# Attention scores of four key tiles accumulated by key differences, values held by chunk, both stored by ScalarE

## The chip, the core and the metric

The kernel runs on one core of one Trainium2 chip. The metric is the device time of one execution in microseconds (us); the median of several runs is compared. A core has TensorE (PE, the matrix multiplier, with its weight loads listed as PEld), VectorE (DVE), ScalarE (ACT), GpSimd (POOL) and SyncE (SP, which here only issues transfers). Each works through its own instructions in order. TensorE writes into banks of PSUM, of 512 fp32 numbers per partition, and may add to what a bank holds. 16 DMA engines move data between SBUF and the chip's memory.

## The reference, cut to what matters

One transformer block with a condition, for `x` of 2 batches, 2048 tokens, width 512, in fp32; 16 heads of 32:

```
mod = silu(cond) @ Wada + bada                    # six vectors per batch
xm  = layernorm(x) * (1 + sc_a) + sh_a
q, k, v = split(xm @ Wqkv)                        # 16 heads of 32
s   = where(causal, q @ k.T * 32**-0.5, -inf)
x   = x + gt_a * (softmax(s) @ v @ Wproj + bproj)
xm  = layernorm(x) * (1 + sc_m) + sh_m
x   = x + gt_m * (gelu(xm @ W1 + b1) @ W2 + b2)
```

## The kernel before, in words

The phases follow each other: QKV of batch 0, attention of batch 0, output projection of batch 0, QKV of batch 1, attention of batch 1, then a last phase with the projection of batch 1 and the MLP.

**QKV** (`Qkv.group`, L811). Tokens are worked in four groups g of 512. In a group, for each of four chunks f (four heads, 128 features) first the queries, then the keys are computed into a PSUM bank `ps_qk` (four matmuls, L823). Each result is split into a high part (ScalarE, L830) and the rest (VectorE, L831), both in a tile `hl` (four buffers), and stored by SP (L836) to scratch in DRAM; after f = 0 the keys of chunk 0 and a block of queries are loaded back (L842). Then four tiles of values `ps_v` are computed and copied by ScalarE into `vv`, which holds the values of all 2048 tokens and 16 heads (L852). `among` is called behind each matmul and sets score products between them (below). `norm` and `load_x` prepare the next group.

In batch 1's QKV, POOL also works on weights for the MLP: `Quarters.step` (L924), and after it `FirstLayer.step` (L988), which loads a room of seven blocks of 512 columns, forms four sums in it and stores it to `w1e` (two rooms, seven of them in all; `also`, L1228, calls them).

**Attention** (`attention_phase`, L541). The keys of a chunk in SBUF (`kst`) and the queries of a unit (`qst`) hold high and low parts on 128 partitions, so that one matmul with 128 rows gives the product of both. A unit is a chunk c and a block i of 512 queries; the order of blocks is 0, 1, 2, 3 in chunk 0 and 0, 2, 1, 3 in the others (L275). A step of a unit is a tile of 128 keys (L662): 4i tiles below the diagonal, then one on it, then two steps for the other three tiles on the diagonal. The exponent needs each query's maximum first. So there are two kinds of products with the keys:

- *Score products* `s` (`Row.score`, L494, through `bank`): queries on the partitions, up to 512 keys wide; VectorE takes the maximum (L461, or L456 with the causal mask). They run ahead, for units to come. They have two PSUM banks, and `score` may borrow one of `st` (`borrow`). How many a step takes is set by `due` and `count` (L675, L484) from the weights of the steps (`weight`, L668) and the costs of the products left.
- *Scores* `st` (`scores_t`, L550): keys on the partitions, 512 queries wide, one bank for each of the four heads. A step first writes minus the maximum into each bank by a small bf16 matmul, the **fold** (`sel` times `fold`, which `rows`, L516, makes), and adds keys times queries. ScalarE takes the exponent into `e` (L593); POOL zeroes what lies above the diagonal (`affine_select`, L602). The loop over the heads in `scores_t` also fixes where a step's score products stand among its scores: behind two or three of them, one more into a borrowed bank at the end.

Two steps later (`LAG`), the products of `e` with the values (`o`) follow (L729). Row sums `sm` come from products with `ones`; for tiles below the diagonal POOL first adds up to five `e` into `ee` (L623; VectorE does so in the last unit), and one product takes the sum (L736). `e` has eight tiles of two heads, `ee` four. `flush` (L656) sets values, row sums and the unit's end behind the scores of the step in which they come due.

Of the kernel before, what the change touches and what calls it, by code (L numbers as in the profile page):

```python
# [12 lines left out]
ALU = mybir.AluOpType  # L13
# [14 lines left out]
def dit_block_kernel(  # L28
# [69 lines left out]
    ones = bp.tile([P, P], F32, tag="ones", name="ones")  # L98
# [8 lines left out]
    nc.vector.tensor_scalar(sel, ones, -1.0, None, ALU.mult)  # L107
# [61 lines left out]
    ]  # L169
    n_early = (C - 1) * NQ  # L170
# [118 lines left out]
    class Row:  # L289


        def __init__(self, b):
            self.b = b
            self.vv = bp.tile([P, NT, D], F32, tag="vv", name="vv")
            self.kst, self.qst, self.pools = {}, {}, {0: bp}
            self.at = 0
# [11 lines left out]
        def load_keys(self, c, g, n=1):  # L308
# [6 lines left out]
            for r in range(4):  # L315
# [3 lines left out]
                )  # L319

# [220 lines left out]
    def attention_phase(row):  # L541
        b, vv, kst, qst = row.b, row.vv, row.kst, row.qst
        with pool(f"att{b}") as ap, pool(
# [4 lines left out]
            n_bank = [0]  # L548

            def scores_t(u, step, n):  # L550
# [21 lines left out]
                for h in range(HC):  # L572
                    g = slice(h * HD, (h + 1) * HD)
                    st = st_bank()
                    mm(
                        st[:, :w], sel[g, :], fold[u % 2][g, q0 : q0 + w],
                        start=True, stop=False,
                    )
                    sts.append(st)
                for h in range(HC):  # L580
                    at = 0
                    for j, q in tiles:
                        mm(
                            sts[h][:, at : at + QB - q],
                            kst[c][:, h, j * P : (j + 1) * P],
                            qst[u][:, h, q:],
                            start=False, stop=at + QB - q == w,
                        )
                        at += QB - q
# [94 lines left out]
            for u, (c, i) in enumerate(units):  # L684
                if NQ <= u + AHEAD < len(units):
                    row.load_queries(u + AHEAD)
                if u % NQ == 0 and c + 1 < C:
                    row.load_keys(c + 1, 0, NG)
                steps = len(steps_of[u])
                for n_step, tiles in enumerate(steps_of[u]):  # L690
                    last = n_step == steps - 1
# [37 lines left out]
                    def values(es=es, tiles=tiles, c=c, o=o, first=n_step == 0, last=last):  # L729
                        tile_by_tile(  # L730
                            o,
                            lambda j, h: vv[:, j, (c * HC + h) * HD : (c * HC + h + 1) * HD],
# [3 lines left out]
                    def row_sums(es, last, tiles=((0, 0),), sm=sm, summed=summed):  # L736
                        first = not summed
                        summed.add(len(summed))
                        tile_by_tile(sm, lambda j, h: ones[:, :HD], es, tiles, first, last)
# [29 lines left out]
    class Qkv:  # L769
# [41 lines left out]
        def group(self, g, hp, between, among):  # L811
# [5 lines left out]
            n = 0  # L817
# [1107 lines left out]
```

## Time and profile before

| | |
|---|---|
| median of 3 runs | 2321.45 us (2317.7 to 2322.69) |
| the profiled execution's own time | 2323.13 us |
| its span | 2321.4 us, mean granted TensorE clock 0.998 |
| PE busy | 2270.8 us (98%) |
| DVE, ACT, POOL busy | 1582.5, 914.6, 1290.9 us |
| DMA | 355.60 MB, mean 153 GB/s |
| QKV, then attention of batch 0 | about 0 to 213, 213 to 742 us |
| projection of batch 0, QKV of batch 1 | about 742 to 826, 826 to 997 us |
| attention of batch 1 | about 997 to 1533 us |
| the rest (projection of batch 1, MLP) | about 1533 to 2321 us |

The profile is of one execution. Its page lists busy times of the engines, slices of the span (a digit is tenths busy, 9 is 90% or more), and groups of instructions: line, engine, operation, tile written and tiles read, shape, count, then busy time, the mean of one in ns, and the engine's idle time just ahead of them with what ended it. A timeline lists start, duration, engine, line and operation in order of time, with the idle time before in brackets and what released it. An x4 joins four like instructions. The time of a matmul in it reaches beyond the start of the next one, since matmuls are pipelined; so the distance of starts is what one costs PE.

### The profile page before, as it was taken

The page shows a single profiled execution, that of the slowest core. Times are in us where ns is not written, and L with a number is a line of the kernel's source. Part 1 is how long each engine was busy: PE and PEld are TensorE (multiplying, and loading weights), DVE is VectorE, ACT ScalarE, POOL GpSimd, SP SyncE. Part 2 cuts the span into 40 slices and gives each one's busy share as a digit, 9 for nine tenths or more (in the row PEclk, how much of TensorE's full clock was granted, in tenths as well). Part 3 has the DMA queues.
Part 4 walks back from the last instruction along what each step waited for, and adds up shares of the span by engine and source line. Part 5 has one row for each costly group of instructions (what it writes and reads, how often), then busy time and mean ns, then how long its engine had stood idle before and what let it go on. Part 6 is the DMA issues. An engine that isn't in the chain of part 4 may idle for free. (4 is left out here: it accounts for less than half of the span.)

```text
span 2321.4 us, 33398 instructions
## 1 busy us (share of the span) xinstructions
PE 2270.8 (98%) x12141; PEld 1388.8 (60%) x12141; DVE 1582.5 (68%) x3117; ACT 914.6 (39%) x1744; POOL 1290.9 (56%) x1036
## 2 busy tenths in 40 slices
PE   8999999999999999999999999999999999999998
PEld 4455545455544444555455554446888888888887
DVE  3366776777666735677667777555896876877787
ACT  2112555555565021155555554622332152251230
POOL 1052987878793663478788886653764602602510
PEclk9999999999999999999999999999999999999999
DMA  7577216151233799981522404265375554654643
GB/s 257 185 243 204 55 28 133 29 119 47 74 115 127 241 297 298 320 235 24 113 48 48 100 24 134 81 206 205 118 279 200 199 186 146 212 173 151 216 143 116
DMA packets 118524, 355.60 MB, mean 153 GB/s; under 512 B 14496, under 2 KB 15052, under 8 KB 103640
## 3 DMA queue, kind: packets, MB, share of 16 engines
q1 hardware_dynamic: 107040, 293.64, 41.9%
q0 software_dynamic: 10944, 59.28, 7.0%
q8 instruction: 96, 1.57, 0.3%
q14 instruction: 68, 0.56, 0.1%
q10 hardware_dynamic: 376, 0.55, 0.1%
HBM read 253.80 MB, written 107.48 MB: 156 GB/s over the span
## 5 line engine op out<-in xcount | busy, mean ns | idle before, releaser
L593 ACT ACTIVATE e<-st 128x512 f32<-128x512 f32 (+1 forms) x1152 | 573.1, 579 | 411.6 <-PE st L203 350.5
L461 DVE TENSOR_REDUCE mx<-s 128x1 f32<-128x512 f32 x604 | 408.0, 687 | 185.0 <-PE s L203 183.6
L623 POOL TENSOR_TENSOR ee<-ee,e 128x1024 f32<-128x1024 f32 x212 | 498.8, 2385 | 8.3 <-ACT e L593 8.3
L203 PE MATMUL s<-kst,qst 128*128 128x512 f32 (+3 forms) x1032 | 466.5, 453 | 15.9 <-DVE mx L461 6.3
L203 PE MATMUL st<-qst,kst 128*128 128x512 f32 (+3 forms) x1280 | 410.1, 387 | 0.0
L203 PE MATMUL ps_a<-sum,room 128*128 128x256 f32 x1504 | 357.4, 382 | 6.6 <-DVE c L1409 3.8
L203 PEld LDWEIGHTS ps_a<-sum,room 128*128 128x128 f32 x1504 | 281.5, 190 | 56.0 <-issue 8.7
L203 PE MATMUL o<-e,vv 128*32 128x512 f32 (+3 forms) x2560 | 300.8, 539 | 0.8 <-POOL e L602 0.8
L203 PEld LDWEIGHTS s<-kst,qst 128*128 128x128 f32 x1032 | 194.5, 189 | 174.0 <-DVE mx L461 58.6
L456 DVE CUSTOM_DVE_ANT_0 junk<-s,causal 128x512 bf16<-128x512 f32 (+3 forms) x428 | 209.2, 489 | 126.2 <-PE s L203 118.7
L203 PEld LDWEIGHTS st<-qst,kst 128*128 128x128 f32 x1280 | 227.5, 188 | 96.8 <-issue 66.7
L623 POOL TENSOR_TENSOR ee<-e 128x1024 f32<-128x1024 f32 x84 | 198.4, 2384 | 130.5 <-ACT e L593 130.4
L203 PE MATMUL ps_qk<-xmT,wqkv 128*128 128x512 f32 x512 | 240.5, 597 | 1.8 <-DVE xmT L263 1.8
L602 POOL TENSOR_SCALAR_AFFINE_SELECT e<-e 128x256 f32<-128x256 f32 x256 | 103.8, 436 | 107.2 <-ACT e L593 74.2
L203 PEld LDWEIGHTS ps_qk<-xmT,wqkv 128*128 128x128 f32 x512 | 94.2, 190 | 97.7 <-issue 91.4
L1637 POOL TENSOR_TENSOR c<-c,h 128x512 f32<-128x512 f32 x40 | 58.2, 1474 | 160.8 <-ACT c L1635 160.8
L203 PE MATMUL ps_b<-sum,room 128*128 128x256 f32 x608 | 143.6, 379 | 0.0
L203 PEld LDWEIGHTS ps_b<-sum,room 128*128 128x128 f32 x608 | 115.0, 190 | 15.4
L203 PE MATMUL ps_v<-wqkv,xmT 128*128 128x512 f32 x256 | 122.3, 594 | 0.0
L203 PEld LDWEIGHTS o<-e,vv 128*32 128x32 f32 x2560 | 60.8, 108 | 101.1 <-issue 83.4
L203 PE MATMUL st<-fold,sel 32*128 32x512 bf16 (+1 forms) x1152 | 116.1, 372 | 3.6 <-DVE mhl L482 2.6
L461 DVE TENSOR_REDUCE mx<-st 128x1 f32<-128x512 f32 x164 | 112.7, 687 | 4.9 <-PE st L203 2.7
(179 smaller groups left out, 2869.6 us busy)
## 6 DMA issues: line engine op xcount, KB each, us to landing
qst<-q SPq DMA_DIRECT2D x128, 256.0 KB
room<-w1e SPq DMA_DIRECT2D x28, 1024.0 KB
kst<-k SPq DMA_DIRECT2D x24, 1024.0 KB
room<-w1e SPq DMA_DIRECT2D x28, 768.0 KB
room<-w2e SPq DMA_DIRECT2D x21, 1024.0 KB
q<-hl SPq DMA_DIRECT2D x32, 512.0 KB
k<-hl SPq DMA_DIRECT2D x32, 512.0 KB
room<-w2e SPq DMA_DIRECT2D x21, 768.0 KB
```

What stands on the lines that cost most here:

```text
L203: return tc.keep_in_program_order(nc.tensor.matmul(*args, **kw))
L456: nc.vector.tensor_tensor_reduce(junk[:, :w], s[:, :w], causal[:, QB - w :], 1.0, MASKED, ALU.add, ALU.max, m,)
L461: nc.vector.tensor_reduce(m, s[:, :w], axis=AX.X, op=ALU.max)
L593: act(nc.scalar.activation(e[:, h % 2, :w], sts[h][:, :w], AF.Exp))
L602: nc.gpsimd.affine_select(d, d, pattern=[[0, 2], [1, P]], compare_op=ALU.is_ge, fill=0.0, base=0, channel_multiplier=-1,)
L623: act(engine.tensor_tensor(dst, x, y, ALU.add))
L1637: nc.gpsimd.tensor_tensor(c, c, piece_of(base, i, t, pair), ALU.add)
```

## The change

Four consecutive key tiles of a 512-key group, below the diagonal, now use the same four banks `st`. The first of the four steps writes the fold and the scores as before. The other three add only (next keys − keys before) times the queries onto the bank that is still there, and so turn the scores of one tile into those of the next, with the maximum already in. Such a step (`by_difference`) has no fold.

- The differences are made in QKV: for g < 3 and each chunk, ScalarE copies 384 columns of the keys' PSUM bank, VectorE subtracts them from the following 384 in the bank, and the difference is split in high and low (`dl`, in the buffers of `hl`, now five) and stored to new scratch `dd` by ScalarE, one tile later. `load_differences` brings them back by SP: those of chunk 0 at the end of each group, those of chunk c + 1 in steps 6, 10 and 14 of the last unit of chunk c.
- The values are held by chunk, in two buffers: chunk 0 is copied in QKV, the other 384 columns go through a tile `vt` (two buffers) to scratch `vd`, stored by ScalarE, and are loaded for the next chunk in the third unit of a chunk.
- The score products of a step with differences stand elsewhere: the first one (with three or more) ahead of its scores, that is, right behind the values of the step before. They borrow no bank, and the step before a step with differences borrows none either. The fixed part of such a step's weight is 800 instead of 1250.
- `ones` has 32 columns; `sel` is made from the identity.
- FirstLayer works in 14 halves of rooms, in three buffers, one call at every n instead of every second one; Quarters' rooms in that stage are three single ones.

The diff, cut to its core:

```
+    dd = [[dram.tile([2, P, NG - 1, MT - P], F32, ...) for c in range(C)] for b in range(B)]
+    vd = [dram.tile([P, NT, D], F32, tag=f"v{b}", name=f"v{b}") for b in range(B)]
...
+        def load_differences(self, c, g):
+            t = bp.tile([P, HC, MT - P], F32R, tag=f"dst{g}", name="dst")
+            for r in range(4):
+                nc.sync.dma_start(
+                    t[r * HD : (r + 1) * HD].bitcast(F32),
+                    dd[self.b][c][r % 2, :, g].rearrange("(h d) t -> d h t", d=HD),
+                )
+            self.dst[c, g] = t
...
+        def new_values(self, c):
+            self.vv[c] = bp.tile([P, NT, P], F32, tag="vv", name="vv", bufs=2)
+        def load_values(self, c):
+            self.new_values(c)
+            nc.sync.dma_start(self.vv[c], vd[self.b][:, :, c * P : (c + 1) * P])
...
+            def by_difference(u, step):
+                return step % TQ > 0 and step < units[u][1] * TQ
...
+                differ = by_difference(u, step)
+                if differ:
+                    sts = banks[0]
+                    first, *behind = {
+                        0: (0, 0, 0, 0, 0),
+                        1: (0, 0, 1, 0, 0),
+                        2: (1, 0, 1, 0, 0),
+                        3: (1, 0, 1, 0, 1),
+                        4: (1, 1, 0, 1, 1),
+                    }[min(n, HC)]
+                    row.score(first)
+                else:
...
+                    banks[0] = sts
...
+                        if differ:
+                            keys = row.dst[c, j // TQ][:, h]
+                            keys = keys[:, (j % TQ - 1) * P : j % TQ * P]
+                        else:
+                            keys = kst[c][:, h, j * P : (j + 1) * P]
                         mm(
+                            sts[h][:, at : at + QB - q], keys, qst[u][:, h, q:],
                             start=False, stop=at + QB - q == w,
+                            skip_group_check=differ,
                         )
...
-                    if h < 2 and n >= 3 or h >= HC - n and n < 3:
+                    if differ:
+                        row.score(behind[h])
+                    elif h < 2 and n >= 3 or h >= HC - n and n < 3:
                         row.score(1)
-                if n >= 3:
-                    row.score(1, st_bank)
+                if n >= 3 and not differ:
+                    row.score(1, None if by_difference(u, step + 1) else st_bank)
                     row.score(min(n, HC) - 3)
...
-                    weight.append(1250 + (12 if n < i * TQ else 14) * w // 2)
+                    fixed = 800 if by_difference(u, n) else 1250
+                    weight.append(fixed + (12 if n < i * TQ else 14) * w // 2)
...
+                if u % NQ == 2 and c + 1 < C:
+                    row.load_values(c + 1)
...
+                    if u % NQ == NQ - 1 and c + 1 < C and n_step in (6, 10, 14):
+                        row.load_differences(c + 1, n_step // TQ - 1)
...
+                    stored(n)
+                    if which and g < NG - 1:
+                        before = hp.tile([P, MT - P], F32, tag="before", name="before")
+                        act(nc.scalar.copy(before, ps[:, : MT - P]))
+                        d = ps[:, P:]
+                        act(nc.vector.tensor_tensor(d, d, before, ALU.subtract))
+                        dl = hp.tile([P, 2, MT], F32R, tag="hl", name="dl", bufs=5)
+                        dl = dl[:, :, : MT - P]
+                        act(nc.scalar.activation(dl[:, 0, :], d, AF.Copy))
+                        act(
+                            nc.vector.tensor_tensor(
+                                dl[:, 1, :], d, dl[:, 0, :].bitcast(F32), ALU.subtract
+                            )
+                        )
+                        late.append((n + 1, dl, f))
...
-                nc.scalar.copy(row.vv[:, g * MTT + t, :], ps)
+                act(nc.scalar.copy(row.vv[0][:, g * MTT + t, :], ps[:, :P]))
+                vt = hp.tile([P, D - P], F32, tag="vt", name="vt", bufs=2)
+                act(nc.scalar.copy(vt, ps[:, P:]))
+                act(nc.scalar.dma_start(vd[b][:, g * MTT + t, P:], vt))
+                stored(n)
```

`stored(n)` lets ScalarE issue the stores of `dl` that are due; `act` keeps an instruction in its place in the program's order.

More of the change, by code (lines that the diff above doesn't have):

```diff
@@ L169, in dit_block_kernel @@
     ]
+    dd = [
+        [
+            dram.tile([2, P, NG - 1, MT - P], F32, tag=f"d{b}{c}", name=f"d{b}{c}")
+            for c in range(C)
+        ]
+        for b in range(B)
+    ]
+    vd = [dram.tile([P, NT, D], F32, tag=f"v{b}", name=f"v{b}") for b in range(B)]
     n_early = (C - 1) * NQ
@@ L738, in row_sums @@
                         summed.add(len(summed))
-                        tile_by_tile(sm, lambda j, h: ones[:, :HD], es, tiles, first, last)
+                        tile_by_tile(sm, lambda j, h: ones, es, tiles, first, last)
                     pending.append((now + LAG, values))
@@ L1231, in also @@
                         quarters.step()
-                elif n % 2 == 0:
+                else:
                     late.step()
             def rooms():
-                w = hp.tile([P, 7, C * P], F32, tag="w49", name="w7", bufs=2)
-                w = w.rearrange("p n d -> p (n d)")
-                return [w[:, k * piece : (k + 1) * piece] for k in range(2)]
+                w = hp.tile([P, 7, HK * P], F32, tag="w49", name="w7", bufs=3)
+                return [w.rearrange("p n d -> p (n d)")]
             quarters.more_rooms = rooms
             qkv.run(hp, also)
-            assert quarters.at >= FC and late.at == 7 and not late.rooms
+            assert quarters.at >= FC and late.at == 14 and not late.rooms
     attention_phase(row)
```

66 lines of the change are left out of this document (41 added, 25 removed).

## The prediction

> **What bounds the kernel now.** I read the page first: its span, the busy line, the slices, the groups.
>
> ```profile
> span 2321.4 us, 33398 instructions
> PE 2270.8 (98%) x12141; PEld 1388.8 (60%) x12141; DVE 1582.5 (68%) x3117; ACT 914.6 (39%) x1744; POOL 1290.9 (56%) x1036
> POOL 1052987878793663478788886653764602602510
> ...
> L623 POOL TENSOR_TENSOR ee<-ee,e 128x1024 f32<-128x1024 f32 x212 | 498.8, 2385 | 8.3 <-ACT e L593 8.3
> L456 DVE CUSTOM_DVE_ANT_0 junk<-s,causal 128x512 bf16<-128x512 f32 (+3 forms) x428 | 209.2, 489 | 126.2 <-PE s L203 118.7
> L203 PE MATMUL st<-fold,sel 32*128 32x512 bf16 (+1 forms) x1152 | 116.1, 372 | 3.6 <-DVE mhl L482 2.6
> ```
>
> TensorE (PE) is full on average; but the slices of POOL (GpSimd) say 8 and 9 tenths for long stretches, and an average over stages hides which of the two ends last. So the windows by stage came next (attention of batch 0, projections and QKV of batch 1, attention of batch 1, then two 10 us pieces inside that QKV; columns: window and length, then PE, PEld, DVE, ACT, POOL busy with counts, granted clock, DMA share, GB/s).
>
> ```profile
> 213.00:742.00 529.00, 521.74 (x3666) 261.55 (x3665) 368.19 (x873) 303.24 (x607) 403.86 (x281) 1.00 0.32 80
> 826.00:997.00 171.00, 166.24 (x468) 82.28 (x466) 90.55 (x218) 30.75 (x55) 84.88 (x106) 0.99 0.93 313
> 997.00:1533.00 536.00, 524.55 (x3666) 262.55 (x3667) 372.16 (x875) 303.63 (x608) 408.42 (x285) 1.00 0.33 85
> ...
> 900.00:910.00 10.00, 7.17 (x16) 3.54 (x17) 6.66 (x16) 0.60 (x1) 2.39 (x3) 0.83 0.86 283
> 930.00:940.00 10.00, 10.00 (x35) 5.38 (x34) 7.50 (x22) 3.28 (x6) 6.12 (x6) 1.00 1.02 368
> ```
>
> Attention has PE busy 98% and the DMA a third busy. QKV of batch 1 is the stage without room: DMA share 0.93, and the one place where PE stops and its clock falls.
>
> The timeline of PE shows what a step of attention costs, and that of DVE (VectorE) how soon a bank of score products comes free.
>
> ```profile
> 652.33 0.39 PE L203 MATMUL st<-fold,sel 32*128 32x512 bf16 x4
> 652.65 0.50 PE L203 MATMUL st<-qst,kst 128*128 128x512 f32 x1
> 652.99 0.40 PE L203 MATMUL s<-kst,qst 128*128 128x512 f32 x1
> ...
> 653.45 0.40 PE L203 MATMUL s<-kst,qst 128*128 128x512 f32 x1
> ...
> 654.15 0.39 PE L203 MATMUL st<-kst,qst 128*128 128x512 f32 x1
> 654.38 0.40 PE L203 MATMUL s<-kst,qst 128*128 128x512 f32 x1
> 654.71 1.06 PE L203 MATMUL o<-e,vv 128*32 128x512 f32 x8
> 655.71 0.39 PE L203 MATMUL st<-fold,sel 32*128 32x512 bf16 x4
> ```
> ```profile
> 653.42 1.29 DVE L461 TENSOR_REDUCE mx<-s 128x1 f32<-128x512 f32 x2 [0.95 <-PE s L203]
> 654.63 0.68 DVE L461 TENSOR_REDUCE mx<-st 128x1 f32<-128x512 f32 x1
> 655.23 0.68 DVE L456 CUSTOM_DVE_ANT_0 junk<-s,causal 128x512 bf16<-128x512 f32 x1
> ```
> ```profile
> 643.89 0.08 DVE L456 DVE_READ_ACCUMULATOR2_ANT mx<- 128x1 f32 x1
> ...
> 644.03 0.19 PEld L203 LDWEIGHTS s<-kst,qst 128*128 128x128 f32 x1 [0.27 <-DVE mx L456]
> ```
>
> A step is 655.71 − 652.33 = **3.38 us**: 0.32 for four folds (652.65 − 652.33), matmuls 0.23 apart (654.38 − 654.15), 1.00 for values and row sums. A reduction starts 0.43 after its product (652.99 to 653.42), reductions follow each other 0.60 apart (654.63 to 655.23), and the next product starts 0.06 after the bank is read (643.97 to 644.03).
>
> **Part 1: the folds.** Steps that differ number 9, 6 and 3 in the units of query blocks 3, 2 and 1: 18 for each of 4 chunks and 2 batches, 144. A fold gone is 0.32, so 144 × 0.32 = 46 us of PE work leave. That is the ceiling. Against it stands where the score products go. By the built order of PE, 18 of the 144 lie in the last units and carry no products, 86 run product, difference, product, two differences, product, difference, product, 38 begin with two products, and 2 have three products. Ahead of differing steps, 42 fold steps end with two products in a row into the two s banks, where one went to a borrowed bank of st before. Replayed by the intervals above, every product 512 wide:
>
> - Plain differing step: products at 0, 0.46, 1.15, 1.61. The second reduction frees its bank at 0.43 + 0.60 + 0.60 + 0.06 = 1.69, so the fourth product waits 0.08. Step 3.38 − 0.32 + about 0.05 = 3.11 at worst, 3.06 without a wait: saves 0.27 to 0.32.
> - Beginning with two products: the third is wanted at 0.69 and its bank is free at 0.43 + 0.60 + 0.06 = 1.09. This and a second wait eat the 0.32 and more: −0.10.
> - The 42 fold steps: their fourth product is wanted at 2.05, its bank is free at 2.35, and more follows in the next step: −0.39.
>
> All wide: 86 × 0.27 − 38 × 0.10 − 42 × 0.39 = +3 us gained. With no bank wait: 124 × 0.32 = 40. The masked reductions (x428, mean 489 ns against the wide 0.68) are shorter; I take −0.02, −0.29 and +0.31, nearer the wide replay because the wide ones are the more: 86 × 0.31 − 38 × 0.02 − 42 × 0.29 = **14 us** that PE could gain.
>
> **Part 2: what POOL allows.** Its timelines over a unit of block 2 (first two rows, 11 steps) and one of block 3 (last three rows):
>
> ```profile
> 365.75 4.73 POOL L623 TENSOR_TENSOR ee<-e 128x1024 f32<-128x1024 f32 x2 [7.36 <-ACT e L593]
> ...
> 399.33 2.20 POOL L602 TENSOR_SCALAR_AFFINE_SELECT e<-e 128x256 f32<-128x256 f32 x6
> ...
> 437.27 9.40 POOL L623 TENSOR_TENSOR ee<-ee,e 128x1024 f32<-128x1024 f32 x4 [0.52 <-ACT e L593]
> 447.92 4.72 POOL L623 TENSOR_TENSOR ee<-e 128x1024 f32<-128x1024 f32 x2 [1.24 <-ACT e L593]
> ...
> 462.58 4.71 POOL L623 TENSOR_TENSOR ee<-e 128x1024 f32<-128x1024 f32 x2 [0.59 <-ACT e L593]
> ```
> ```profile
> 401.55 0.16 PEld L203 LDWEIGHTS o<-e,vv 128*32 128x32 f32 x8 [0.23 <-POOL e L602]
> ```
>
> In block 2 POOL runs without a gap from 365.75 to 401.53 (399.33 + 2.20; the rows between name no idle time), and at its end PE already waits 0.23 for the diagonal's selects, which stand in POOL's queue behind the adds. The adds don't change. A faster PE arrives at the same select and waits longer: **block 2 with its 48 differing steps gains nothing**. In block 3 POOL idles 0.52 + 1.24 + 0.59 = 2.35 us; only that can be taken. Six such units (the last units add on DVE) hold 6 × 2.35 = 14 us at most; I take the largest single idle of each, 1.24, since a chain's first add still waits for its own Exp: −7.4 us.
>
> Something goes back. Of the units of blocks 2 and 3, 12 have a first differing step that begins with two products. There the second head's difference comes behind the waiting third product: 0.23 × 3 + 0.40 + 0.23 + 0.06 of DVE order = about 1.38 after the values, against 652.99 + 0.23 − 652.33 = 0.89 now. POOL's first add and all behind it start 0.49 later: 12 × 0.49 = +5.9. Attention with products: −7.4 + 5.9 = **−1.5** (bounds: −14, that idle all used and nothing given back; +20, the wide losses of the 42 and 38 steps, 16.4 + 3.8, with no step's gain).
>
> **Part 3: the last units.** No products stand there, and DVE adds.
>
> ```profile
> 704.48 0.40 PE L203 MATMUL st<-fold,sel 32*128 32x512 bf16 x4
> ...
> 706.93 0.40 PE L203 MATMUL st<-fold,sel 32*128 32x512 bf16 x4
> ```
> ```profile
> 705.39 2.06 ACT L593 ACTIVATE e<-st 128x512 f32<-128x512 f32 x4 [0.39 <-PE st L203]
> ```
>
> A step is 2.45; without the fold 2.13, still over the 2.06 of ACT (ScalarE). At most 18 × 0.32 = 5.8; but the same four banks are written again, each only after its Exp, so ACT's chain nearly closes. I take **−4** (bounds −5.8 and 0).
>
> **Part 4: QKV.** Per group with g < 3 there are new: 4 ACT copies and 4 high parts of 384, 4 × 2 subtractions on DVE, 4 stores by ScalarE; per V tile a second copy and a store; then 4 loads of differences on SP. DMA per batch, by the tiles' sizes: 12 × 393 KB of differences (4.7 MB), 16 × 196 KB of values (3.1 MB), 3 × 786 KB loaded back (2.4 MB): 10.2 MB. The loads for later chunks lie in attention, at a DMA share of a third; I price them at nothing there, and at 2 us for a batch if that cover failed. FirstLayer moves the same bytes in halves, in three rooms. In batch 0 QKV the DMA has gaps and DVE is not full; I take **+2** (0 to +6).
>
> In batch 1 the cover is thin. What waits there, and for what, by the waits of that stage and the timelines of PE and POOL:
>
> ```profile
> POOL w L968 <- DMA w1e<-w: 42.2, 5, 12.7
> DVE stat L215 <- DMA x<-in_x_dram: 13.7, 6, 4.7
> SPq L316 <- DMA k<-hl: 17.3, 3, 10.3
> ...
> ACT hl L830 <- DMA k<-hl: 0.9, 1, 0.9
> ```
> ```profile
> 902.83 0.50 PE L203 MATMUL s<-kst,qst 128*128 128x512 f32 x1 [3.17 <-DVE mx L461]
> ```
> ```profile
> 1000.54 0.58 POOL L996 DMA_DIRECT2D w1e<-w  x1 [0.30 <-POOL w L963]
> 1001.13 2.28 POOL L602 TENSOR_SCALAR_AFFINE_SELECT e<-e 128x256 f32<-128x256 f32 x6
> ```
>
> One late x tile stops DVE, in whose queue the reductions stand behind it; so PE stands for 3.17 us, and runs the 10 us around it at clock 0.83 (another 1.7). The stores of differences stand ahead of such loads on the same DMA engines: 313 GB/s × 171 us are 53.5 MB, so 10.2 MB is 19% more traffic, and each of the 6 late x tiles comes later by about that share of 10 us, SP's longest wait here, taken as the age of a transfer that queues: 6 × 1.9 = 11, of which I let a third reach PE, as 3.17 + 1.7 of 13.7 did: +4. The buffer hl serves 12 tiles of a group in place of 8: five buffers for a tile each 2.5 us instead of four for one each 3.76, 12.5 us of cover instead of 15, while SP stands up to 10.3 us before it can store: +2. POOL's rooms end 0.6 us ahead of the attention's first selects; the same traffic stretches them: +3. Together **+9** (0, if DMA and DVE hide all, to +29, under the rivals).
>
> On the stores: the row of the DMA share says 1.02 at 930. The Trainium skill (DMA: Bandwidth & Descriptors, section Issuing engines are not separate DMA queues) says that transfers of all issuing engines run on the same 16 DMA engines and interleave, so that another issuer saves only issue time. By it, storing from ScalarE spares SP 28 issues a batch and nothing on the engines; were it otherwise, the +4 for x would be 0. No run here shows it yet.
>
> MLP: unchanged, 0.
>
> **Sum:** −1.5 − 4 + 2 + 9 = +5.5 on the profiled execution's 2323.13: 2328.6. That execution lies 1.7 above the median of the shown runs (2321.45), so the median to expect is **2327**.
>
> **Rivals.**
> *Faster: PE's bound is the real one.* The banks do not bind and POOL's idle is used: 6 × 2.35 + 5.8 in the last units = 20, less 2 for QKV, where gaps of the DMA hide the rest: 2321.45 − 18 = 2303. For it: masked reductions are short, POOL has 125 us idle in the 529. Against: those lie at units' starts, and 401.55 shows POOL ending last. Chance 0.27.
> *Slower: DMA in QKV of batch 1.* 10.2 MB at 368 GB/s take 28 us, and a share of 0.93 leaves 0.07 × 171 = 12: 16 over. When a tile in hl lives over 12.5 us (SP's 10.3 and the landing), ACT stops, with it DVE and the products: 3 groups × 4.5 = 13. It decides from the point where landings pass 2.2 us behind SP's longest wait. −5.5 + 2 + 29 = +25.5: 2347. For it: 1.02 at 930. Against: 0.86 at 900 leaves gaps. Chance 0.20.
> *It doesn't show:* POOL's and DVE's slack return what the folds give and QKV hides all but 2: −5.5 + 2 = 2318. Chance 0.15.
>
> **How the numbers follow.** Forecast 0.38 (own range 2320 to 2334). About 0.2% (4.6 us) is what a measurement here can tell from none. Forecast gives 0.24 slower, 0.14 same; the DMA rival 0.20 slower; the quiet one 0.09 same, 0.06 faster; the fast one 0.27 faster. Sum: faster 0.33, same 0.23, slower 0.44. Range 2302 to 2346: about one tenth left out at each end, half of either extreme rival.
>
> **What would show it.** Plain differing steps of 3.06 to 3.11 in PE's timeline, and fold steps before them 0.3 longer with PEld waiting for DVE mx (part 1). PE's waits for POOL's selects grow from 0.23 to 1 us and more in block 2, its unit's length unchanged (part 2); if POOL ends first there, the fast rival holds. Last units at 2.13 to 2.25 a step. In QKV of batch 1 the waits for x and hl and the stage's length, +9. I am wrong if the attention windows move by over 15 us or QKV's by over 15.

## The result and the profile after

The changed kernel takes 2381.1 us (median of 4 runs, 2378.14 to 2382.82) against 2319.57 of the kernel before: 1.0263 times as long, 95% interval 1.0245 to 1.0281. Slower by 61.5 us, where 2327 was forecast.

The page of after, in the lines that answer to those of before; the row of the products' weight loads is added, first of before, then of after:

```profile
L203 PEld LDWEIGHTS s<-kst,qst 128*128 128x128 f32 x1032 | 194.5, 189 | 174.0 <-DVE mx L461 58.6
```
```profile
span 2381.1 us, 32561 instructions
PE 2274.6 (96%) x11565; PEld 1370.1 (58%) x11565; DVE 1612.1 (68%) x3165; ACT 945.0 (40%) x1824; POOL 1312.0 (55%) x1078
POOL 1042787778865564658878777845566512412410
...
L672 POOL TENSOR_TENSOR ee<-ee,e 128x1024 f32<-128x1024 f32 x212 | 498.5, 2385 | 9.2 <-ACT e L640 9.1
L211 PEld LDWEIGHTS s<-kst,qst 128*128 128x128 f32 x1198 | 224.7, 190 | 340.7 <-DVE mx L487 165.0
L482 DVE CUSTOM_DVE_ANT_0 junk<-s,causal 128x128 bf16<-128x128 f32 (+3 forms) x480 | 233.5, 486 | 115.0 <-PE s L211 106.6
```

The 576 folds are gone, but PE works no less (2270.8 to 2274.6 us), and weight loads of score products wait 165.0 us for the reduction that frees their bank, where they waited 58.6.

The stages, cut at the first fold, the first output projection and the first `ps_qk` of each batch (us; the experiments, e1 to e14, are told below and stand beside, each from its one profiled execution):

| | QKV b0 | attention b0 | projection b0 | QKV b1 | attention b1 | rest | span |
|---|---|---|---|---|---|---|---|
| before | 213.4 | 529.0 | 57.9 | 196.6 | 536.0 | 788.5 | 2321.4 |
| after | 234.8 | 540.9 | 58.0 | 213.3 | 547.9 | 786.2 | 2381.1 |
| e1 scores as before | 237.0 | 528.3 | 57.2 | 210.4 | 536.5 | 783.5 | 2352.9 |
| e2 attention alone | 214.3 | 541.6 | 57.4 | 197.1 | 553.9 | 783.7 | 2348.0 |
| e3 half maxima, after | 231.9 | 520.6 | 57.9 | 214.3 | 526.4 | 784.5 | 2335.6 |
| e4 half maxima, before | 212.6 | 524.7 | 56.9 | 192.4 | 539.0 | 785.2 | 2310.8 |
| e5 values only | 215.5 | 528.4 | 57.4 | 198.3 | 546.7 | 785.9 | 2332.2 |
| e6 differences unstored | 218.4 | 529.4 | 57.3 | 197.3 | 545.0 | 786.3 | 2333.7 |
| e7 stores by SP | 230.4 | 531.4 | 57.6 | 223.4 | 537.3 | 786.3 | 2366.4 |
| e8 product among values | 234.9 | 606.1 | 57.7 | 211.1 | 610.7 | 783.7 | 2504.2 |
| e9 last units only | 215.8 | 526.9 | 57.4 | 199.3 | 534.0 | 783.4 | 2316.8 |
| e10 the same, full values | 214.0 | 526.9 | 57.5 | 199.2 | 533.5 | 785.5 | 2316.6 |
| e11 first loads late | 213.9 | 528.9 | 58.0 | 205.4 | 537.8 | 787.4 | 2331.4 |
| e12 own buffers | 216.6 | 528.9 | 57.3 | 201.7 | 546.5 | 787.4 | 2338.4 |
| e14 first loads late, full change | 214.8 | 541.3 | 57.9 | 207.7 | 551.3 | 783.9 | 2356.9 |
| e13 fold steps spread | 215.9 | 536.2 | 57.9 | 211.8 | 562.9 | 784.1 | 2368.8 |

The loss is 21.4 + 11.9 + 0.1 + 16.7 + 11.9 − 2.3 = 59.7 us of span: 38 in QKV, 24 in attention.

Attention by kind of step, mean us a step and score products in brackets, each step from PE's timeline (the first start behind one step's values to the first behind the next's), both batches, steps paired one to one:

| | count | before | after | e4 | e3 | e14 | e13 |
|---|---|---|---|---|---|---|---|
| differing, one product first | 88 | 3.74 (376) | 3.64 (350) | 3.75 | 3.47 | 3.64 | 3.64 |
| differing, two products first | 38 | 4.06 (174) | 4.42 (190) | 4.03 | 4.15 | 4.42 | 4.41 |
| fold steps ahead of differing | 42 | 3.64 (178) | 4.02 (168) | 3.59 | 3.71 | 3.99 | 3.85 |
| last units, differing | 18 | 3.02 (0) | 2.60 (0) | 3.02 | 2.60 | 2.60 | 2.60 |
| the others | 98 | 3.82 (360) | 3.93 (380) | 3.83 | 3.89 | 3.97 | 4.11 |

Row by row after minus before: −9.0, +13.6, +16.0, −7.5, +10.7: +23.8. The first two rows are the 126 steps that lost their fold and have products: together they take 4.6 us longer. A plain differing step of after, all products wide, in PE's timeline and in that of its weight loads:

```profile
404.76 0.50 PE L211 MATMUL s<-kst,qst 128*128 128x512 f32 x1
405.09 0.40 PE L211 MATMUL st<-qst,dst 128*128 128x512 f32 x1
405.32 0.39 PE L211 MATMUL s<-kst,qst 128*128 128x512 f32 x1
405.56 0.62 PE L211 MATMUL st<-qst,dst 128*128 128x512 f32 x2
406.04 0.51 PE L211 MATMUL s<-kst,qst 128*128 128x512 f32 x1
406.38 0.40 PE L211 MATMUL st<-qst,dst 128*128 128x512 f32 x1
406.63 0.49 PE L211 MATMUL s<-kst,qst 128*128 128x512 f32 x1
407.06 1.06 PE L211 MATMUL o<-e,vv 128*32 128x512 f32 x8
408.05 0.50 PE L211 MATMUL s<-kst,qst 128*128 128x512 f32 x1
```
```profile
404.75 0.19 PEld L211 LDWEIGHTS s<-kst,qst 128*128 128x128 f32 x1 [0.84 <-DVE mx L487]
404.86 0.19 PEld L211 LDWEIGHTS st<-qst,dst 128*128 128x128 f32 x1
405.09 0.19 PEld L211 LDWEIGHTS s<-kst,qst 128*128 128x128 f32 x1
...
406.03 0.19 PEld L211 LDWEIGHTS s<-kst,qst 128*128 128x128 f32 x1 [0.29 <-DVE mx L487]
...
406.63 0.19 PEld L211 LDWEIGHTS s<-kst,qst 128*128 128x128 f32 x1 [0.30 <-DVE mx L487]
```

And weight loads of the old step, none of which waits for a reduction:

```profile
652.65 0.19 PEld L203 LDWEIGHTS st<-qst,kst 128*128 128x128 f32 x1 [0.23 <-issue]
652.76 0.19 PEld L203 LDWEIGHTS s<-kst,qst 128*128 128x128 f32 x1
652.99 0.19 PEld L203 LDWEIGHTS st<-qst,kst 128*128 128x128 f32 x1
```

In the old step the weights of `s` are loaded at 652.76, 0.23 ahead of their matmul at 652.99, and matmuls follow each other by 0.23. In the new one the product at 404.76 has its load at 404.75: the load stands behind the wait for the bank, so nothing was loaded ahead, and the next matmul comes after 0.33 (405.09). That happens three times (at 404.76, 406.04 and 406.63, each drawn with 0.5 in place of 0.4), 0.10 each. The old step has one such load too, behind its folds: 652.65, with the next matmul at 652.99. So two more in the new step take 0.20 of the fold's 0.32, and the waits themselves some 0.04: the step takes 408.05 − 404.76 = 3.29 us, not 3.06 to 3.11, against 3.38 with its fold. It isn't this step alone. In both attentions of after, 156 wide matmuls whose load waited for a maximum have their next matmul 0.34 us later (median), and 753 with the load ahead 0.23; in before 219 whose load came late with no wait that the profile shows ("issue") have it 0.34 later as well.

### The profile page after: what moved, and what is told of

Read it like the earlier page. It is cut to its first block, busy times and chain, and to the rows that moved or that the text cites. A ratio compares the mean times of both kernels' runs of the same rounds, so it can differ in the third digit from the quotient of the medians.

```text
span 2381.1 us, 32561 instructions
## 1 busy us (share of the span) xinstructions
PE 2274.6 (96%) x11565; PEld 1370.1 (58%) x11565; DVE 1612.1 (68%) x3165; ACT 945.0 (40%) x1824; POOL 1312.0 (55%) x1078
## 4 chain that ended last, share of the span: by engine, by line
PE 81%; DVE 10%; DMA 4%; issue 2%; POOL 1%; ACT 1%; ACTq 0%; SPq 0%; DVEq 0%; POOLq 0%
PE ps_a L211 14%; PE s L211 12%; PE st L211 12%; PE o L211 11%; PE ps_qk L211 7%; PE ps_b L211 7%; PE ps_o L211 4%; PE sm L211 4%; PE ps_v L211 4%; PE ps_c L211 4%; DVE mx L487 3%; DMA d<-dl 1%; DVE sum L1380 1%; PE ps_xt L219 1%; DVE junk L482 1%
## 5 line engine op out<-in xcount | busy, mean ns | idle before, releaser
L487 DVE TENSOR_REDUCE mx<-s 128x1 f32<-128x512 f32 x718 | 482.9, 689 | 234.1 <-PE s L211 229.0
L211 PE MATMUL s<-kst,qst 128*128 128x512 f32 (+3 forms) x1198 | 556.5, 472 | 52.1 <-DVE mx L487 23.5
L211 PEld LDWEIGHTS s<-kst,qst 128*128 128x128 f32 x1198 | 224.7, 190 | 340.7 <-DVE mx L487 165.0
L482 DVE CUSTOM_DVE_ANT_0 junk<-s,causal 128x128 bf16<-128x128 f32 (+3 forms) x480 | 233.5, 486 | 115.0 <-PE s L211 106.6
L672 POOL TENSOR_TENSOR ee<-e 128x1024 f32<-128x1024 f32 x84 | 198.3, 2383 | 153.3 <-ACT e L640 153.3
L211 PE MATMUL ps_qk<-xmT,wqkv 128*128 128x512 f32 x512 | 248.6, 614 | 1.8 <-DVE xmT L271 1.8
L211 PE MATMUL st<-qst,dst 128*128 128x512 f32 x576 | 200.5, 402 | 0.0
L211 PE MATMUL st<-qst,kst 128*128 128x512 f32 (+2 forms) x704 | 199.9, 360 | 0.0
L211 PEld LDWEIGHTS st<-qst,kst 128*128 128x128 f32 x704 | 121.6, 189 | 44.2 <-issue 29.4
L211 PEld LDWEIGHTS ps_b<-sum,room 128*128 128x128 f32 x608 | 115.0, 190 | 15.4
L211 PEld LDWEIGHTS st<-qst,dst 128*128 128x128 f32 x576 | 105.7, 189 | 24.9 <-ACT e L640 11.9
L1028 POOL DMA_DIRECT2D w<-in_L_cond_W_dram x64 | 41.0, 663 | 143.0 <-DMA d<-dl 118.6
```

What stands on the lines that cost most here:

```text
L211: return tc.keep_in_program_order(nc.tensor.matmul(*args, **kw))
L482: nc.vector.tensor_tensor_reduce(junk[:, :w], s[:, :w], causal[:, QB - w :], 1.0, MASKED, ALU.add, ALU.max, m,)
L487: nc.vector.tensor_reduce(m, s[:, :w], axis=AX.X, op=ALU.max)
L672: act(engine.tensor_tensor(dst, x, y, ALU.add))
L1028: nc.gpsimd.dma_start(w[:, n], src)
```

## Experiments in attention

**e1: scores as before.**

```
-                return step % TQ > 0 and step < units[u][1] * TQ
+                return False
```

> The changed kernel with by_difference never true: every step of attention has its fold and its old products; the differences are still made, stored and loaded, but not used, and the values stay by chunk. If the attention's loss (after minus before: +11.8 us in each of the two) comes from the order of products and folds itself, attention is back at 529 and 536 us and QKV stays at 234.9 and 213.3: about 2381 - 24 = 2357 us. If it comes from the added loads and stores (DMA share 0.32 to 0.40 in attention), attention stays near 541 and 548 and the time near 2381.

2355.5 us, 1.0145 (1.0115 to 1.0175). Attention is back at 528.3 and 536.5 with all loads still there, QKV stays late. So the attention's loss is made by the new order of its own PE work, not by traffic.

**e2: attention alone.** QKV's block from `if which and g < NG - 1` on, `stored` and `vt` are taken out.

```
-                    dd[self.b][c][r % 2, :, g].rearrange("(h d) t -> d h t", d=HD),
+                    qd[self.b][c][r % 2, :, g * MT + P : (g + 1) * MT].rearrange(...),
...
-            nc.sync.dma_start(self.vv[c], vd[self.b][:, :, c * P : (c + 1) * P])
+            nc.sync.dma_start(self.vv[c], qd[self.b][c][0].rearrange("p (n t) -> p n t", t=P))
```

> The changed attention alone: QKV makes and stores no differences and copies only 128 value columns; the differences and the values of later chunks are loaded in the same sizes from the queries' scratch (so the scores and values are not the block's), chunk 0's differences at the start of attention. If the QKV loss (+21.4 and +16.7 us) lies in what QKV makes and stores, QKV is back at 213.4 and 196.6 us and the time is 2381 - 38 = 2343 us, attention still about +11.8 each. If the attention's loss was only handed on from QKV, the time is about 2320 us or lower.

2350.29 us, 1.0131 (1.0099 to 1.0164): QKV back at 214.3 and 197.1, attention +12.6 in batch 0. The two losses are separate. In batch 1 attention is longer by 17.9, 6 more than expected, and 6.4 of the 17.9 lies in its first three steps; e5 shows why.

**e3 and e4: half maxima.**

```
-                nc.vector.tensor_reduce(m, s[:, :w], axis=AX.X, op=ALU.max)
+                nc.vector.tensor_reduce(m, s[:, : w // 2], axis=AX.X, op=ALU.max)
```

> The changed kernel with the unmasked maxima taken over half the columns (the other half left out), so that such a reduction takes about 0.35 us in place of 0.60 from one to the next. If the waits of score products for their two banks eat the folds, attention is 25 to 45 us shorter (both batches together) than in the same variant of the kernel before, steps that differ take 3.06 us or less, and fold steps ahead of them 3.4. If POOL is what holds the steps, it is at most 20 us shorter, with longer waits for the selects.

> The kernel before with the same half maxima (the other half left out): the baseline for the run above. Its steps have little to wait for, so both theories expect attention within 10 us of 529 + 536 us.

One run each: 2337.35 and 2312.58 us. With shorter reductions the changed attention is 20.3 and 21.5 us shorter, 41.8 in all; the attention before is 4.3 shorter in batch 0 and 3.1 longer in batch 1. The same shortening is worth far more to the changed order, and more than its whole loss of 23.8. Against e4, e3 is 4.1 and 12.6 shorter, 17 in all, less than the 25 expected of the bank theory and within the 20 allowed to POOL; 5.5 of the 12.6 is e4's own, in two early steps of batch 1 where PE waits up to 3.06 us for POOL's selects. The step table tells the theories apart: fold steps ahead of differing ones fall from 4.02 to 3.71, those with two products first from 4.42 to 4.15, those with one from 3.64 to 3.47, while e4's steps stay where before's are. Plain all-wide differing steps (twelve in each run) have a median of 3.31 in after and 3.05 in e3, within 0.01 of the 3.06 that the prediction had for a step without a wait. The waits of weight loads over attention of batch 0, before, after, then e3:

```profile
PEld s L203 <- DVE mx L461: 25.0, 37, 1.0
...
PEld s L203 <- DVE mx L456: 15.2, 24, 0.8
...
PEld o L203 <- POOL e L602: 6.2, 15, 0.9
```
```profile
PEld s L211 <- DVE mx L487: 74.2, 160, 1.4
...
PEld s L211 <- DVE mx L482: 33.5, 58, 0.8
...
PEld o L211 <- POOL e L649: 9.0, 17, 2.3
```
```profile
PEld s L211 <- DVE mx L487: 40.9, 61, 0.9
...
PEld s L211 <- DVE mx L482: 29.4, 53, 0.8
...
PEld o L211 <- POOL e L649: 12.1, 29, 2.3
```

Each row gives the sum in us, the number of waits and the longest. The waits for unmasked maxima (L461, then L487) tripled and fall to 40.9 in e3; those for POOL's selects change by 3 us. POOL is not what holds the steps with products. That half maxima do not bring all of the folds back fits the masked maxima (L456, then L482), whose waits doubled and which e3 does not shorten (29.4), and the products moved between kinds of steps; no run divides these.

**e8: a product among the values.** No two products in a row, about 0.7 us apart.

```
+                        5: (1, 1, 0, 1, 1), 4: (1, 0, 1, 0, 1),
...
             def products(dst, lhs, es, q0, at, first, last):
                 for h in range(HC):
+                    if h == 2:
+                        row.score(mid[0])
+                        mid[0] = 0
```

> The changed kernel with the score products of steps that differ, and of the fold step ahead of them, set about 0.7 us apart: one stands between the second and third of the four products of values (or row sums), and no two follow each other. If two banks and the 0.60 us from one reduction to the next eat the folds, the losses of after (fold steps ahead +16.0, steps that begin with two products +13.6 us, both batches) vanish and attention is 529 + 536 less 25 to 40 us: about 515 and 520, and the time about 2337. If POOL holds the steps, attention is not below 525 and 530, and PE's waits for the selects grow. If the position doesn't matter, attention stays at 541 and 548.

2513.21 us, 1.083 (1.0808 to 1.0853); attention 606.1 and 610.7, as no theory had it. PE's timeline of e8, the values behind a differing step and the product among them:

```profile
430.37 1.05 PE L211 MATMUL o<-e,vv 128*32 128x512 f32 x4
431.35 0.49 PE L211 MATMUL s<-kst,qst 128*128 128x512 f32 x1
431.77 1.05 PE L211 MATMUL o<-e,vv 128*32 128x512 f32 x4
432.76 0.50 PE L211 MATMUL s<-kst,qst 128*128 128x512 f32 x1
```

Half of the values takes 0.98 us (430.37 to 431.35), as long as all of them in after (407.06 to 408.05, x8). The rows name weights of 128*32, one head's 32 columns; that two heads take as long as four says that the heads run at the same time. Cut in two, the group is paid twice. The run says nothing of the products' place; it says that this block cannot be cut.

**e14 and e13: the fold steps' products.** Both have the loads of chunk 0's differences at attention's start in the program (see e11); e13 also changes the fold steps ahead of differing ones.

```
+                    if n >= HC and by_difference(u, step + 1):
+                        first, behind = 1, (1, 0, 1, 1)
```

> The full change, with chunk 0's differences loaded at the start of attention (as in e11) and nothing else altered. If those loads, standing ahead of x on SP, cost QKV of batch 0 its 21.4 us, it is back at 213 to 216, QKV of batch 1 at 205 to 208, attention still about +12 in each: 2381 - 21 - 7 = 2353. If they now collide with attention's start, or QKV depended on something else, 2365 or more.

> As e14, and the fold steps ahead of a differing step place four products as the differing steps do: one, a score, one, two scores, one, a score, one, so that no two follow each other at the end. By the replay with two banks such a step loses 0.05 instead of 0.39; after measured +0.38 a step, 16.0 us for 42. If that place is the cause, these steps return to 3.6 to 3.7 and attention falls by 12 to 16 us in all: about 2339. If the two banks only pass the wait on to the differing steps behind, these grow and the sum stays within 4 us of e14.

e14: 2358.62 us, 1.0165 (1.015 to 1.0181). e13: 2357.63 us, 1.0142 (1.0111 to 1.0173), with runs from 2347.1 to 2370.55. The changed steps fall from 3.99 to 3.85, 42 × 0.14 = 6 us, about half of the least expected, and differing steps do not grow; attention of batch 0 is 5.1 shorter. So the place explains a part (6 of 15 us). The rest of that kind's loss goes with the two banks at any place, as far as e3 says (3.71 there with shorter reductions); no run gives these steps a third bank. e13's median can't be told from e14's: its profiled execution is the slowest of its four, and attention of batch 1 was 11.6 longer in it, all of that in its first steps:

```profile
1040.96 2.87 POOL L1056 TENSOR_TENSOR w<-w 128x256 f32<-128x256 f32 x4 [11.68 <-DMA w<-w1d]
...
1044.92 3.06 POOL L653 TENSOR_SCALAR_AFFINE_SELECT e<-e 128x256 f32<-128x256 f32 x8
```
```profile
1045.57 2.27 PE L211 MATMUL o<-e,vv 128*32 128x512 f32 x8 [13.35 <-POOL e L653]
```

POOL waited 11.68 us for a room of FirstLayer, and attention, begun at 1021.8, stood 13.35 us for POOL's selects. In e14 the same wait for a room is 6.99 us, and attention of batch 1 is 3.4 longer than in after.

## Experiments in QKV

**e5: values only; e6: differences made, not stored.** From e1, e5 drops the differences, e6 their stores and loads.

```
-                    _, dl, f = late.pop(0)
-                    act(nc.scalar.dma_start(dd[b][f]..., dl.bitcast(F32)))
+                    late.pop(0)
```

> As e1 (scores as before), and the differences are not made, stored or loaded; values by chunk stay, with their stores by ScalarE, and FirstLayer's halves stay. In e1 QKV took 237.0 and 210.4 us against 213.4 and 196.6. If the values' part (second copies, stores through two buffers vt, 3.1 MB a batch) carries a good share, QKV stays 5 us or more above before in each batch; if the differences carry it all, QKV is at 213 to 215 and 196 to 199, and the time about 2321.

> As e1, but the differences are made by ScalarE and VectorE and neither stored nor loaded; values by chunk stay. Against e5 it shows the work on the engines, against e1 the transfers with the hold they keep on the buffers hl. If engine work makes QKV late (VectorE's queue, in which the reductions and the norm stand), QKV stays within 5 us of e1's 237.0 and 210.4; if stores and loads do, it is within 5 us of e5's.

e5: 2331.67 us, 1.0043 (1.0028 to 1.0058); QKV +2.1 and +1.7. e6: 2335.47, 1.0069 (1.0046 to 1.0093); QKV 218.4 and 197.3. So second copies and subtractions cost 5 us at most in batch 0 and under 1 in batch 1; 18.6 and 13.1 us come with stores and loads. Both pay elsewhere: attention of batch 1 is 10.7 and 9.0 longer. POOL in e5, with attention begun at 999.6:

```profile
1007.86 2.91 POOL L1033 TENSOR_TENSOR w<-w 128x256 f32<-128x256 f32 x4 [3.38 <-DMA w<-w1d]
1011.06 0.95 POOL L1073 DMA_DIRECT2D w1e<-w  x1 [0.30 <-DVE mx L487]
1011.85 3.07 POOL L649 TENSOR_SCALAR_AFFINE_SELECT e<-e 128x256 f32<-128x256 f32 x8
```

The last store of FirstLayer is at 1011.06, 11.5 us into attention; before it was at 1000.54, 3.6 us into it. Fourteen halves end some 10 us later than seven whole rooms, and the first selects stand behind them: 6.3 of e5's 10.7 and 7.8 of e6's 9.0 lie in the first three steps of attention. In after this is hidden, because QKV itself ends at 1047.0. e9 and e10, with whole rooms, do not have it.

**e7: stores by SP.** From e1.

```
-                        nc.scalar.dma_start(
+                        nc.sync.dma_start(
                             dd[b][f][:, :, g].rearrange("l p t -> p l t"), dl.bitcast(F32)
...
-                act(nc.scalar.dma_start(vd[b][:, g * MTT + t, P:], vt))
+                act(nc.sync.dma_start(vd[b][:, g * MTT + t, P:], vt))
```

> As e1, with the stores of differences and values issued by SP in place of ScalarE. The transfers stay on the same 16 engines. If only they matter, QKV is within 4 us of e1's 237.0 and 210.4. If the issues in ScalarE's own order (0.34 to 0.46 us each, and what stands behind them) make the loss, QKV is 10 us or more shorter per batch; if SP becomes the jam, since its loads wait for stores, QKV is longer.

2368.54 us, 1.0205 (1.0178 to 1.0233): QKV 230.4 and 223.4, 6.6 shorter than e1's in one batch and 13.0 longer in the other. ScalarE's issues make at most 6.6 us of the loss. In batch 1 SP is late: it asks for the stage's two x groups 59.7 and 117.3 us after the stage's start, where e1 does at 48.8 and 102.9.

**e11: first loads late.** From e1.

```
-                if f == C - 1 and g < NG - 1:
-                    row.load_differences(0, g)
...
+                    if u == 0 and n_step == 0:
+                        for g in range(NG - 1):
+                            row.load_differences(0, g)
```

> As e1 (scores as before, differences made, stored, loaded, values by chunk), with chunk 0's differences loaded at the start of attention, so that their twelve loads no longer stand on SP ahead of the next group's x. If SP's order makes x late, QKV falls from e1's 237.0 and 210.4 by 6 us or more in batch 0; if the buffers hl or the traffic decide, by less than 4.

2334.93 us, 1.0058 (1.0038 to 1.0078). QKV of batch 0 is at 213.9, all of its loss gone, with every store still made; batch 1 is 5.0 shorter. On the chip the moved loads don't all wait for attention: SP issues ten of the twelve within QKV of batch 0, from 153.75 us on, but none of them ahead of an x. The issues of SP: in before, in after, in e11.

```profile
114.55 2.29 SPq L781 DMA_DIRECT2D x<-in_x_dram  x4
```
```profile
124.73 3.59 SPq L333 DMA_DIRECT2D dst<-d  x4
...
129.98 2.16 SPq L835 DMA_DIRECT2D x<-in_x_dram  x4
```
```profile
114.67 2.29 SPq L838 DMA_DIRECT2D x<-in_x_dram  x4
```

In after, the same group's x is asked for 15.4 us later, behind the loads of differences. The group itself began 9.5 us late (its first `ps_qk` is at 118.6, against 109.1), because the group before had been served likewise: its x, too, stood behind four loads, and PE stood 5.26 us for it. What that does, in PE's timeline and in the windows of after (columns as before):

```profile
151.60 2.12 PE L219 MATMUL ps_xt<-ident,x 128*128 128x128 f32 x8 [5.81 <-DVE x L252]
```
```profile
140.00:160.00 20.00, 14.19 (x48) 8.15 (x46) 14.48 (x37) 3.59 (x7) 10.40 (x14) 0.83 1.01 265
...
151.60:155.10 3.50, 3.50 (x11) 2.38 (x11) 2.32 (x5) 1.13 (x2) 2.53 (x4) 0.50 1.05 253
```

PE stands 5.81 us for the normalized x, and over 20 us its granted clock is 0.83. Part of that falls into the idle time; behind it PE works 3.5 us at a clock of 0.50, an estimated 3.5 × 0.5 = 1.8 us more. The Trainium skill (TensorE: Matmul & The Clock Gate, section HAM oscillation — how this bites in real kernels) warns of gaps over some 3.4 us that throttle PE; these rows agree, but the gap of 3.17 us that the prediction shows, a little shorter, went with 0.83 over 10 us as well. Of the 21.4 us, 4.6 falls into the last group, behind whose loads no x follows; e11 has it gone too, and which of SP's other issues makes it isn't shown. e14 shows the same for the full change: 214.8, against 234.8.

**e12: own buffers.** From e11.

```
-                        dl = hp.tile([P, 2, MT], F32R, tag="hl", name="dl", bufs=5)
+                        dl = hp.tile([P, 2, MT - P], F32R, tag="dl", name="dl", bufs=4)
...
-                vt = hp.tile([P, D - P], F32, tag="vt", name="vt", bufs=2)
+                vt = hp.tile([P, D - P], F32, tag="vt", name="vt", bufs=4)
```

> As e11, and the differences have four buffers of their own (hl four, as before), vt four in place of two; the differences' loads lie in attention's own memory. The stores and their bytes are the same. If what e1 loses over e6 (18.6 and 13.1 us) is the wait for a buffer whose store has not landed, QKV falls to e6's 218 and 197 to 200; if it is the traffic itself, it stays within 5 us of e11.

2336.35 us, 1.0064 (1.0042 to 1.0087): QKV 216.6 and 201.7. Batch 1 gains 3.7 over e11, and FirstLayer's tail takes more than that back (attention 546.5, 8.7 longer than in e11, 5.7 of it in the first three steps); batch 0 gains nothing. The hold on the buffers, `hl`'s and `vt`'s together, is a small part; what is left in batch 1 (201.7 − 196.6 = 5 us) is not divided further between traffic and engines.

## A version that keeps what works

**e9 and e10: differences in the last units alone,** where no score products stand; FirstLayer and rooms as before, in e10 values too.

```
-                return step % TQ > 0 and step < units[u][1] * TQ
+                return u == len(units) - 1 and step % TQ > 0 and step < units[u][1] * TQ
...
-                    if which and g < NG - 1:
+                    if which and g < NG - 1 and f == C - 1:
```

> The changed kernel with key differences in the last unit of each batch alone, where no score products stand: only those of chunk 3 are made, stored and loaded (a quarter of the stores), FirstLayer and its rooms as before, values still by chunk. In after, the 18 steps of the last units gave 7.5 us and all others lost 31. If the lost gain lies in the products' banks, attention is 529.0 - 3.7 and 536.0 - 3.7 us; QKV, by e5 (+2) and a quarter of the rest, +4 to +7 a batch: about 2320 - 7.5 + 11 = 2323. If differences themselves cost attention (banks held, loads), its two stages are not shorter than before.

> As e9, but with all values in SBUF as before (no stores or loads of values), and the differences loaded key tile by key tile into four small buffers. Attention as in e9 if those loads are in time, 525 and 532 us; QKV has only a quarter of the differences, +1 to +4 a batch by the stores' share in e1 (18 and 13 us for all). About 2320 - 7.5 + 5 = 2317.5, down to 2313 if QKV hides them. If a small loss of DMA or queue order decides in QKV whatever its size, it is 2320 or more.

e9: 2318.36 us over 10 runs, 0.9986 (0.9977 to 0.9995). e10: 2319.09 over 12, 0.9997 (0.9986 to 1.0009). Both stages of attention gain 2.0 to 2.5, less than the 3.7 expected; QKV gives 0.6 to 2.7 a batch back. PE in e9's last unit, then in its last step, and in the last step of before:

```profile
706.38 1.19 PE L211 MATMUL st<-qst,dst 128*128 128x512 f32 x4
707.50 1.07 PE L211 MATMUL o<-e,vv 128*32 128x512 f32 x8
708.50 0.39 PE L211 MATMUL st<-fold,sel 32*128 32x512 bf16 x4
...
737.13 2.48 PE L211 MATMUL o<-e,vv 128*32 128x384 f32 x11 [1.43 <-POOL e L651]
```
```profile
735.83 3.55 PE L203 MATMUL o<-e,vv 128*32 128x512 f32 x19
```

A step without fold takes 708.50 − 706.38 = 2.12 us, where one took 2.45. The missing 1.4 us is in the last step: PE comes to that step's values 1.2 us earlier (734.64, against 735.83), but POOL's selects start no earlier (735.68, against 735.44), and PE stands 1.43 us for them. That step takes 8.92 us in place of 7.49, by the same 1.4 in both batches of e9, e10 and after. Here POOL does cap the gain. e9 beats both kernels, if barely; e10 cannot be told from before.

## Why the prediction was wrong

- **Part 1 failed, in its replay.** It priced a product that finds its bank busy by the wait alone. Each also loses 0.10, since its weights could not be loaded ahead; a plain step has three such, the old one one. It forecast +0.31 a plain step, +14 us in all; the runs gave 0.10 a step, part of it because 26 products fewer stand there (26 × 0.23 = 6 us of 9.0), and a loss with the other kinds. Its wide replay had fold steps at −0.39, which was right (−0.38), but −0.29 went into the sum; steps with two products first were set at −0.02 and took 0.36 more. The 98 others, set at nothing, took 0.11 more: 4.6 of their 10.7 us is 20 products moved into them (20 × 0.23), 2.8 the last steps' waits for POOL.
- **Part 2 named the wrong bound.** POOL's idle and its selects were to cap the gain. In the steps with products there was none to cap: with attention 20 us shorter, e3's weight loads waited 3 us more for selects in batch 0 (9.0 to 12.1). The attention term was −1.5 − 4; measured +11.9 a batch with the last units in it. Without the 18 steps of the last units that is +31 (23.8 + 7.5) for both, or some 28 without the last steps too, beyond the bound of +20.
- **Part 3 was right in its total by luck.** It forecast −4 for both batches, and e9 gives −4.1, e10 −4.6. But the steps themselves gave 18 × 0.42 = 7.5, beyond the bound of −5.8: 0.33 a step comes from the fold, and one step of each batch is 1.13 shorter (4.11 to 2.98). What took the rest back was not ScalarE's chain, as forecast, but POOL's selects in the last step.
- **Part 4 failed for batch 0,** set at +2 because the DMA has gaps there: +21.4. What decided was not room on the DMA engines but the place of twelve loads on SP, eight of them ahead of the next group's x. The prediction counted these loads' bytes and not what stands behind them on their queue. For batch 1, +9 was low: +16.7, of which the same loads are 5 to 6 (e11, e14); the rival's mechanism, the buffers, is about 4 there (e12, `hl`'s and `vt`'s together). The last 5 stay open.
- **The rule cited there** from the Trainium skill (DMA: Bandwidth & Descriptors, section Issuing engines are not separate DMA queues) isn't contradicted by e7: with the stores at another issuer the two QKV stages took 453.8 us together, in e1 447.4. That transfers of two issuers interleave no run here shows. Yet the order on one issuer's queue matters by more than issue time: twelve loads, 3.59 us of issue for each four and eight of them ahead of an x, cost a stage 21 us.
- **The rivals:** the slower one looked at QKV of batch 1 alone and gave 2347. None had attention slower for PE's own reasons; only the bound of +20 in part 2 allowed for it.

## What to carry to other kernels

Before work is moved into an engine's gaps, ask what each moved instruction waits for: a matmul whose load stands behind a wait costs more than the wait. In a plain step two more of these took two thirds of what four cheap folds gave, and in the steps around it the waits took more than all of it. Of each new transfer, look at what stands behind it on its issuing queue, not only at its bytes. A saving pays first where nothing else competes, here in the last units; try it there alone.

## What was not expected of the hardware

- Values of four heads, 32 columns each, take 0.98 us together, and two of them take as long (e8): a group of narrow matmuls is one price, and an instruction set between them doubles it. The Trainium skill (TensorE: Matmul & The Clock Gate, section Part 3: Packing small matmuls — row/col tiling) says that such matmuls run at the same time; the trace agrees.
- A weight load of 128 rows does run while the matmul ahead of it is on (652.76, beside the matmul from 652.65); one that waits for a maximum costs 0.10 us beyond its wait (0.34 to the next matmul in place of 0.23), and so does one that is late for a reason the profile doesn't show.
